# Attention to the context: a new order of scores, sums and fills on TensorE, with the sums of values kept in SBUF

## The chip, the cores and the metric

The kernel runs on one core of a Trainium2 chip. The metric is the device time of one execution in microseconds; lower is better. A time is the median of several runs; views of the profile come from one further execution.

## The reference

The model is a stack of four layers of attention to a context, self-attention and a feed-forward block on x, 2 x 256 tokens of 256 features in float32. The change touches the attention to the context of layers 0 and 1. The context has 2 x 4096 tokens. Layer 0, cut to what matters (layer 1 is the same with other weights, no biases, and a projection of the output):

```python
q = _split_heads(hidden_states @ q_w.T + q_b)      # 16 heads of 16 features
k = _split_heads(context @ k_w.T + k_b)
v = _split_heads(context @ v_w.T + v_b)
scores = jnp.einsum('bhqd,bhkd->bhqk', q, k) / jnp.sqrt(jnp.float32(HD))
mask = (attention_mask > 0)[:, None, None, :]
scores = jnp.where(mask, -jnp.inf, scores)
probs = jax.nn.softmax(scores, axis=-1)
ctx = jnp.einsum('bhqk,bhkd->bhqd', probs, v)
```

Layer 3 attends to the context in another way. It needs, for each context token, a projection of its features, a softmax of the powers of their logarithms and, for each head, the 11 largest of 16 features (`_topk_sparsify`). Then it sums features times context over all tokens:

```python
k = k @ Wk.T
k = _focus(k, focusing_factor)      # |.|, mean, softmax(log * factor)
kh = _topk_sparsify(_to_heads(k))   # 11 of 16
kv = jnp.einsum('bnc,bnd->bcd', kh / sqrt_l, vh / sqrt_l)
```

This does not depend on x, and the kernel does it in the loops of layers 0 and 1 (one batch each), beside their attention.

## The kernel before

A layer's loop has 8 units (2 batches, 4 chunks of 4 heads) of 16 steps each (`PER`). A unit goes twice over the keys of its 4 heads, which lie as 32 rows each in the 128 partitions. Its first pass, `first_scores` (L1145), multiplies queries by keys, 4 matmuls of 32 x 128 weights and 512 keys a step, and VectorE takes the maximum of each bank (L1163). When the unit is through, `shift_queries` puts the maximum of each query into a spare row of the queries. The second pass, `scores` (L1169), runs 18 steps behind (`PER + LAG`): scores by key, 8 matmuls of 32 x 128 weights and 256 queries, then on ScalarE three exponentials (L1188), two of 512 elements and one of 1024. `weigh` (L1190) runs another step behind: 8 matmuls with 128 x 32 weights (values) add into one PSUM bank over the whole unit, four heads in four column tiles; the sum is copied out after 16 steps (L1210). `inverses` and `normalize` (L1135) divide it. TensorE does each float32 matmul in two passes, so the profile counts two instructions for each.

Beside these, a step has at most one fill: `project_keys` (L1066, two key chunks in two column tiles of 64, 8 matmul instructions, copied by ScalarE and stored by DMA into the key tiles), `project_values` (L1108), `Focus.project` (L752, one or two tiles of 128 tokens, copied by ScalarE) or `Focus.add_up` (L782, the sum of features times context, added by VectorE at L793). The first and last of these use `Net.matmuls` (L184) with full 128 x 128 weights; so do the values.

What follows the features is done in small pieces. `magnitudes` (L632) makes four ScalarE instructions and one of GpSimd for each tile. `weigh` of `Focus` (L641) takes logarithms (two loads of ScalarE's tables around them), multiplies on GpSimd and takes exponentials. `sparsify` (L671) finds the rank of each feature by 45 VectorE instructions and a few around them.

PE, VectorE and ScalarE run in the order in which the program issues (`manual_schedule`, L468). In `attend` (L1013) a step issues: s1 with its maxima; the fill; pieces of the ranking; s2 with its exponentials; the magnitudes of the features taken; weigh of the step before; pieces of `Focus.weigh`. Where the fills and the pieces of ranking go is worked out by `plan` (L896) from deadlines (a key tile, a value tile is due before its step) and from a credit of VectorE time: a step has room for 2.0 us of ranking, or 2.75 with a long fill, less what else VectorE does in it.

PSUM has 8 banks: here 3 of `mm` (in turn for the two single banks of a pair of scores, and for fills), 2 pairs of `sc` (the other two banks of a set of scores), 1 of `acc` (the values' sum).

Of the kernel before, what the change touches and what calls it, by code (L numbers as in the profile page):

```python
# [9 lines left out]

# [9 lines left out]
F32 = mybir.dt.float32  # L20
# [50 lines left out]
class Net:  # L71
# [43 lines left out]
    def four(self, name):  # L115

        ones, pair = [self.mm(name) for _ in range(2)], self.sc(name)
        banks = [*ones, pair[:, 0], pair[:, 1]]
        return banks, [(0, ones[0].unsqueeze(1)), (1, ones[1].unsqueeze(1)), (2, pair)]
# [64 lines left out]
    def matmuls(self, out, pairs):  # L184

        for i, (lhsT, rhs) in enumerate(pairs):
            self.nc.tensor.matmul(out, lhsT=lhsT, rhs=rhs, start=i == 0, stop=i == len(pairs) - 1)  # L187

# [282 lines left out]
    def attend_to_context(self, a, x, q_bias, wq, wo, alive):  # L471
        tc = self.tc
        with self.stage():
            norm = self.center(self.halves(x))
            if not a.begun:
                a.beginning = a.begin(2)
                run(a.beginning, 1)
            a.take_queries(norm, wq, q_bias, alive)
        with (
            self.banks(mm=3, sc=2, acc=1),  # L480
            tc.tile_pool(name="xa_v", bufs=1, reuse_waits="tile") as vpool,
            tc.tile_pool(name="xa_p", bufs=1, reuse_waits="tile") as ppool,
            tc.tile_pool(name="focus", bufs=2, reuse_waits="tile") as fpool,
        ):
            a.attend(vpool, ppool, fpool)
        with self.stage():
            return a.give_back(x, wo)
# [124 lines left out]
class Focus:  # L612
# [139 lines left out]
    def project(self, kc, first, n=1):  # L752
# [12 lines left out]
        for i in range(n):  # L765
# [5 lines left out]
            net.matmuls(ps[:, i * D : (i + 1) * D], [(ctx[:, d, at], self.wk[:, d, :]) for d in range(ND)])  # L771
# [3 lines left out]
        yield  # L775
# [6 lines left out]
    def add_up(self, kc, m):  # L782
# [3 lines left out]
        ps = self.net.mm("kc_sum")[:, : D + 1]  # L786
        self.net.matmuls(ps, [(k[:, t, m * P : (m + 1) * P], self.tokens[:, t, :]) for t in range(NT)])
        yield
        kc_sum = self.kc[self.b][:, m, :]
# [4 lines left out]
        if m == ND - 1:  # L794
            self.load_tokens()


class ContextAttention:
# [36 lines left out]
    def begin(self, n):  # L835
# [5 lines left out]
        for j in range(n):  # L841
            run(self.project_keys(j))
            yield
# [52 lines left out]
    def plan(self):  # L896

        PER, LAG, n = self.PER, self.LAG, len(self.UNITS)  # L900
        STEPS = (n + 1) * PER + LAG + 2
        focus = self.net.focus
        fills, todo, kinds, last = {}, [], {}, n * PER
        self.done = {}

        short, full = 2.0, 2.75
        taken = [0.0] * (STEPS + 8)
        for u in range(n):
            at = PER * (u + 1)
            fills[at] = self.shift_queries(u)  # L910
            taken[at - 1] += 0.3
            taken[at] += 0.43
            at = PER * (u + 2) + LAG + 1
            self.done[at] = u
            taken[at - 1] += 0.43
            taken[at] += 0.25
            if u < n - 1:
                fills[at + 1] = self.normalize(u)
                taken[at + 1] += 0.43 if self.v_bias is None else 0.8

        for kc in range(NKC):
            first = 5 + 31 * kc // 2
            todo += [(first + 2 * t + 4, first + t, ("features", kc, t)) for t in range(NT)]
            todo += [(first + 29.5 + m, first + 14, ("sums", kc, m)) for m in range(ND)]
        for j in range(self.begun, n * NKC // 2):
# [3 lines left out]
            free = max(4 * j - 8, 2 * i + PER + LAG + 1 if i >= 0 else 0)  # L929
            todo.append((4 * j - (5 if j < NKC // 2 else 3), free + 1, ("keys", j)))  # L930
        for b in range(NB):
            for kc in range(NKC):
                for k2 in range(2):
                    i = b * NKC + kc - self.VALUE_TILES
                    free = (i // NKC + 1) * NC16 * PER + LAG + 2 * (i % NKC) + 2 if i >= 0 else -1
                    first = (b * NC16 + 1) * PER + LAG + 2 * kc + k2
                    todo.append((first, free + 1, ("values", b, kc, k2)))
        todo.sort()
        fixed = sorted(fills)
        make = dict(keys=self.project_keys, values=self.project_values, features=focus.project, sums=focus.add_up)  # L940
        self.weighings, self.rankings, costs = {}, {}, focus.costs()
        begin, over, logs, credit = {}, {}, set(), 0.0
        ranked, at, waiting = 0, 0, []
# [11 lines left out]
        def ready(g, deadline, earliest, which):  # L955
            kind, kc, *_ = which
            if earliest > g or (g in logs and kind != "sums" and deadline > g):
                return False
            if kind == "keys":

                return kinds.get(g - 1) != kind or deadline <= g
            if kind == "features":
                return kc < 3 or not any(w[:2] == ("sums", kc - 3) for _, _, w in todo)
            return kind != "sums" or over.get(kc, g) + 1 < g

        def pressed(g):

            for n, (deadline, _, _) in enumerate(todo):
                if n + 1 + sum(g < f <= deadline for f in fixed) > deadline - g:
                    return True  # L970
            return False

        for g in range(STEPS):
            room = short
            t = None if g in fills else next((t for t in todo if ready(g, *t)), None)
            if t is not None:
                todo.remove(t)
                kind, *which = t[2]
                kinds[g] = kind
                assert t[0] >= g or kind in ("features", "sums"), (g, t)  # L980
                fills[g] = make[kind](*which)
                if kind == "features":
                    kc, tile = which
                    if tile + 1 < NT and pressed(g):
                        todo.remove(next(t for t in todo if t[2] == ("features", kc, tile + 1)))
                        fills[g] = focus.project(kc, tile, 2)
                        room, tile = full, tile + 1
                    if tile == NT - 1:
                        waiting.append((kc, g))
                else:  # L990
                    room = full
                    taken[g] += 0.42 * (kind == "sums")

                    if kind == "sums" and waiting and waiting[0][1] < g - 1:
                        take_logs(g - 1)
            if g < PER:
                room = 0.5
            if g >= last + 1:
                room = 2.2
            if waiting and waiting[0][1] < g and (ranked == waiting[0][0] or ranked + 1 == waiting[0][0] and at >= 30):  # L1000
                take_logs(g)
            credit = min(credit, 0.5) + room - taken[g]
# [7 lines left out]
        assert not todo and ranked == NKC, (todo, ranked)  # L1010
        return fills

    def attend(self, vpool, ppool, fpool):  # L1013
# [12 lines left out]
        for g in range((n + 1) * PER + LAG + 2):  # L1026
            second = g - PER - LAG
            if g < n * PER:
                self.first_scores(g // PER, g % PER)
# [6 lines left out]
            run(fills.get(g, ()))  # L1036
# [5 lines left out]
            if 0 <= second < n * PER:  # L1042
                self.scores(second // PER, second % PER)
            focus.magnitudes_of_taken()
            if 0 <= second - 1 < n * PER:
                self.weigh((second - 1) // PER, (second - 1) % PER)
            if g in self.done:
                self.inverses = net.inverses(self.weighed)
                if self.done[g] == n - 1:
                    run(self.normalize(n - 1))  # L1050
# [15 lines left out]
    def project_keys(self, j):  # L1066
# [5 lines left out]
        dense = self.cpool.tile([P, KC], F32, name="k_dense", tag="k_dense")  # L1072
        ps = net.mm("k_ps")
        for d in range(ND):
            for i, ctx in enumerate(self.key_ctx[j]):
                nc.tensor.matmul(  # L1076
                    ps[i * HR : (i + 1) * HR, :],
                    lhsT=self.wk[:, d, c * HR : (c + 1) * HR],
                    rhs=ctx[:, d, :],
                    start=d == 0,  # L1080
                    stop=d == ND - 1,
                )
            if d < ND - 1:
                yield
        self.load_keys_ctx()
        if self.k_bias is None:
            nc.scalar.copy(dense, ps)
        else:
            nc.scalar.activation(dense, ps, AF.Identity, bias=self.k_bias[:, c : c + 1])
# [18 lines left out]
    def project_values(self, b, kc, k2):  # L1108

        net, nc = self.net, self.nc  # L1110
        if k2 == 0:
# [5 lines left out]
        for kk in range(2):  # L1117
            at = slice(kk * P, (kk + 1) * P)
            net.matmuls(ps[:, kk * D : (kk + 1) * D], [(ctx[:, d, at], self.wv[:, d, :]) for d in range(ND)])
            if kk == 0:  # L1120
                yield
        heads = v[:, 2 * k2 : 2 * k2 + 2, : H * VH].rearrange("p k (h e) -> p k h e", e=VH)
        nc.scalar.copy(heads[:, :, :, :DH], ps.rearrange("p (k h e) -> p k h e", k=2, e=DH))  # L1123
        self.load_values_ctx()

    def shift_queries(self, u):
# [5 lines left out]
        yield  # L1132
        nc.vector.tensor_tensor(self.q[u], self.q[u], ps[:, :S], ALU.add)

    def normalize(self, u):  # L1135
# [6 lines left out]
        yield  # L1142


    def first_scores(self, u, n):  # L1145
# [16 lines left out]
        for i, sc in parts:  # L1162
            nc.vector.tensor_reduce(mx[:, qt, i : i + sc.shape[1], kc], sc, AX.X, ALU.max)  # L1163
# [26 lines left out]
    def weigh(self, u, n):  # L1190
# [4 lines left out]
        if n == 0:  # L1195
            self.acc = self.net.acc("attn_acc")
        ps, v = self.weights.pop((u, n)), self.values[b, kc]
        for kk in range(2):
            for i in range(NG):
                at = (c * NG + i) * VH  # L1200
                nc.tensor.matmul(  # L1201
                    self.acc[i * HP : (i + 1) * HP, :S],
                    lhsT=v[:, 2 * k2 + kk, at : at + HP],
                    rhs=ps[:, i, kk * S : (kk + 1) * S],
                    start=n == kk == 0,
                    stop=n == self.PER - 1 and kk == 1,
                )
        if n == self.PER - 1:
            self.weighed = self.ppool.tile([P, S], F32, name="a", tag="a")
            nc.vector.tensor_copy(self.weighed, self.acc[:, :S])  # L1210
# [1160 lines left out]
```

## Time and profile before

| | before |
|---|---|
| median of 3 runs, us | 2444.99 (2443.58 to 2449.97) |
| profiled execution, us | 2444.92 |
| its span from first to last instruction, us | 2443.2 |
| PE busy, us (share) | 2288.8 (94%) |
| VectorE (DVE) busy | 1546.0 (63%) |
| ScalarE (ACT) busy | 1115.1 (46%) |
| GpSimd (POOL) busy | 347.3 (14%) |
| mean granted clock of TensorE | 0.966 |
| chain that ended last: PE, DVE, ACT | 56%, 5%, 3% |
| layer 0's loop: s1 alone, all three, without s1 | 65.1, 536.4, 49.4 us |
| layer 1's loop, the same | 55.7, 535.6, 48.9 us |

Busy time of PE counts pipelined matmuls, so a full PE is not one at its peak. A line of the groups has the source line, the engine, the operation, what it writes and reads, its shape and count, then busy time and mean ns of one, then the idle time of its engine ahead of it and what ended most of that. A line of the timeline has start, duration, engine, line, operation, shape and count. PEld is the load of weights, which runs beside PE.

### The profile page before, as it was taken

Reading aid. Unit: us, or ns where it says so; the run is one execution under the profiler, and the core shown is the slowest. Engines: PE = TensorE matmul, PEld = TensorE weight load, DVE = VectorE, ACT = ScalarE, POOL = GpSimd, SP = SyncE. Lnnn points to the kernel's source line nnn. Section 1 sums busy time; section 2 is a strip of 40 time slices with the busy share of each in tenths; the row PEclk is TensorE's granted clock in tenths of the full one; section 3 lists DMA queues with packets and bytes.
Section 4 is the critical chain, followed back from the end, with each engine's and each line's share of the span. In section 5 each row is a group of like instructions: output and inputs, shape, how many; then the busy total and the mean of one; then the engine's idle time right before and its main releaser. Section 6 shows DMA issues by size and latency. Waiting matters only on the chain.

```text
span 2443.2 us, 43313 instructions
## 1 busy us (share of the span) xinstructions
PE 2288.8 (94%) x17142; PEld 1228.1 (50%) x17142; DVE 1546.0 (63%) x2947; ACT 1115.1 (46%) x2185; POOL 347.3 (14%) x529
## 2 busy tenths in 40 slices
PE   7999999999999699999999999999999996899998
PEld 3454444544544365544454544564448453455453
DVE  4978988788746657978888778453331354444343
ACT  3466655655715334556566566641131252233232
POOL 4000001000024603000010010000011031003030
PEclk9999999999999799999999999999999997898989
DMA  6432232132011123332222221201323100000100
GB/s 200 147 98 86 93 97 93 54 114 67 10 39 36 50 95 120 102 97 92 93 92 93 76 89 41 79 23 52 100 94 95 43 19 14 35 21 12 59 12 22
DMA packets 97801, 174.45 MB, mean 71 GB/s; under 512 B 15120, under 2 KB 63888, under 8 KB 96704
## 3 DMA queue, kind: packets, MB, share of 16 engines
q1 hardware_dynamic: 97600, 171.68, 21.8%
q8 instruction: 137, 2.24, 0.4%
q14 instruction: 64, 0.52, 0.1%
HBM read 154.25 MB, written 0.59 MB: 63 GB/s over the span
## 4 chain that ended last, share of the span: by engine, by line
PE 56%; DVE 5%; ACT 3%; POOL 1%; issue 1%; DMA 0%; ACTq 0%; SPq 0%; DVEq 0%; POOLq 0%
PE s L1179 6%; PE s L1155 5%; PE proj L187 5%; PE attn_acc L1201 5%; PE v_ps L187 4%; PE expert L187 2%; PE k_ps L1076 2%; PE s L187 2%; PE c_acc L1799 2%; PE ffn_ps L187 2%; PE s L1476 1%; PE f_ps L187 1%; DVE mx L1163 1%; PE kc_sum L187 1%; PE kq_ps L187 1%; PE qk_ps L187 1%
## 5 line engine op out<-in xcount | busy, mean ns | idle before, releaser
L1163 DVE TENSOR_REDUCE mx<-s 128x1 f32<-128x512 f32 (+1 forms) x768 | 619.7, 863 | 189.6 <-PE s L1155 187.9
L1188 ACT ACTIVATE p<-s 128x512 f32<-128x512 f32 (+1 forms) x768 | 512.1, 740 | 233.6 <-PE s L1179 232.5
L1179 PE MATMUL s<-xa_q,xa_k 32*128 32x256 f32 x4096 | 338.4, 401 | 22.6 <-DVE mx L1163 22.6
L1155 PE MATMUL s<-xa_k,xa_q 32*128 32x512 f32 x2048 | 313.7, 640 | 5.7 <-ACT p L1188 3.6
L1179 PEld LDWEIGHTS s<-xa_q,xa_k 32*128 32x128 f32 x4096 | 212.9, 184 | 161.5 <-DVE mx L1163 104.1
L1201 PE MATMUL attn_acc<-p,xv 128*32 128x256 f32 x4096 | 277.7, 385 | 0.6 <-ACT p L1188 0.6
L1201 PEld LDWEIGHTS attn_acc<-p,xv 128*32 128x32 f32 x4096 | 111.9, 109 | 128.2 <-issue 83.2
L685 DVE TENSOR_TENSOR ge<-fy 128x960 bf16<-128x960 f32 (+14 forms) x240 | 169.6, 707 | 6.5
L639 POOL TENSOR_TENSOR fy<-fy,low 128x256 f32<-128x256 f32 x64 | 46.4, 725 | 844.5 <-ACT fy L638 844.5
L1155 PEld LDWEIGHTS s<-xa_k,xa_q 32*128 32x128 f32 x2048 | 88.7, 183 | 121.4 <-ACT p L1188 66.7
L687 DVE TENSOR_TENSOR rank<-rank,ge 128x960 bf16<-128x960 bf16 (+14 forms) x240 | 103.9, 433 | 6.0
L689 DVE TENSOR_TENSOR rank<-rank,ge 128x960 bf16<-128x960 bf16 (+14 forms) x240 | 100.9, 421 | 2.6
L395 POOL TENSOR_SCALAR p<-p,r 128x128 f32<-128x128 f32 (+1 forms) x192 | 82.5, 442 | 130.5 <-DVE r L391 70.6
L1123 ACT COPY xv<-v_ps 128x512 f32<-128x512 f32 x64 | 37.6, 587 | 115.7 <-PE v_ps L187 114.1
L376 ACT ACTIVATE p<-p,top 128x256 f32<-128x256 f32 (+1 forms) x128 | 57.1, 447 | 70.1 <-DVE top L364 68.9
L1076 PE MATMUL k_ps<-ctx_k,w_L0x_wk 128*64 128x512 f32 x256 | 66.7, 615 | 6.5 <-DMA ctx_k<-in_ctxT 6.1
L187 PE MATMUL f_ps<-f_wk,f_ctx 128*128 128x256 f32 x256 | 68.9, 400 | 0.6 <-DMA f_ctx<-in_ctxT 0.6
L187 PEld LDWEIGHTS f_ps<-f_wk,f_ctx 128*128 128x128 f32 x256 | 44.5, 189 | 43.2 <-ACT p L1188 19.0
L1799 PE MATMUL c_acc<-pT,ctx_n 128*128 128x256 f32 x256 | 62.0, 387 | 4.2 <-ACT pT L1772 3.0
L187 PE MATMUL v_ps<-w_L0x_wv,ctx_v 128*128 128x256 f32 x256 | 64.8, 397 | 0.0
L187 PE MATMUL kc_sum<-f_tok,fy 128*128 128x257 f32 x256 | 64.2, 393 | 0.0
L187 PE MATMUL v_ps<-w_L1x_wv,ctx_v 128*128 128x256 f32 x256 | 63.8, 392 | 0.0
(489 smaller groups left out, 3353.1 us busy)
## 6 DMA issues: line engine op xcount, KB each, us to landing
ctx_k<-in_ctxT SPq DMA_DIRECT2D x128, 512.0 KB
ctx_v<-in_ctxT SPq DMA_DIRECT2D x64, 256.0 KB
xa_k<-k_dense SPq DMA_DIRECT2D x512, 32.0 KB
f_ctx<-in_ctxT SPq DMA_DIRECT2D x32, 256.0 KB
f_tok<-in_ctx SPq DMA_DIRECT2D x16, 512.0 KB
ctxT<-in_ctxT SPq DMA_DIRECT2D x16, 512.0 KB
ctx_n<-in_ctx SPq DMA_DIRECT2D x16, 512.0 KB
xa_k<-key_masks SPq DMA_DIRECT2D x128, 8.0 KB
```

What stands on the lines that cost most here:

```text
L187: self.nc.tensor.matmul(out, lhsT=lhsT, rhs=rhs, start=i == 0, stop=i == len(pairs) - 1)
L395: nc.gpsimd.tensor_scalar(p[:, j, :nk], p[:, j, :nk], r[:, j : j + 1], 1.0, ALU.mult, ALU.mult)
L685: nc.vector.tensor_tensor(ge[:, :, :n], w[:, :, :n], w[:, :, P - n :], ALU.is_ge)
L687: nc.vector.tensor_tensor(rank[:, :, P - n :], rank[:, :, P - n :], ge[:, :, :n], ALU.add)
L689: nc.vector.tensor_tensor(rank[:, :, :n], rank[:, :, :n], ge[:, :, :n], ALU.subtract)
L1076: nc.tensor.matmul(ps[i * HR : (i + 1) * HR, :], lhsT=self.wk[:, d, c * HR : (c + 1) * HR], rhs=ctx[:, d, :], start=d == 0, stop=d == ND - 1,)
L1155: nc.tensor.matmul(banks[i], lhsT=self.q[u][rows, qt * P : (qt + 1) * P], rhs=k[rows, :], start=True, stop=True,)
L1163: nc.vector.tensor_reduce(mx[:, qt, i : i + sc.shape[1], kc], sc, AX.X, ALU.max)
L1179: nc.tensor.matmul(banks[i][:, kk * S : (kk + 1) * S], lhsT=k[rows, at], rhs=self.q[u][rows, :], start=True, stop=True,)
L1188: nc.scalar.activation(p[:, i : i + sc.shape[1], :], sc, AF.Exp, scale=DH**-0.5)
L1201: nc.tensor.matmul(self.acc[i * HP : (i + 1) * HP, :S], lhsT=v[:, 2 * k2 + kk, at : at + HP], rhs=ps[:, i, kk * S : (kk + 1) * S], start=n ...
L1799: nc.tensor.matmul(accs[m], lhsT=of[:, (k + i) % (KC // P), m * P : (m + 1) * P], rhs=pT[:, i, :], start=k + i == 0, stop=k + i == KT - 1,)
```

## The change

- The order of a step becomes: s2 with its exponentials; s1 with the maxima of its two single banks; weigh of the step before; the maximum of s1's pair of banks (a function of its own now); the fills; pieces of the ranking; magnitudes; pieces of `Focus.weigh`.
- The values, features and sums are multiplied by `by_columns`: each matmul with 128 columns of weights becomes four with 32, in four column tiles. The keys go in four tiles of 32 columns and not in two of 64.
- `weigh` takes an `mm` bank in each step, closes its sum there, and VectorE adds it to a tile in SBUF (a copy in a unit's first step). The bank of `acc` goes to `mm`, which has 4.
- A fill is cut into two parts (a half of the keys, one of two token tiles, a half of the columns of a sum); a step gets none, one or several of them, after the largest share of parts per step that any deadline asks for.
- The planner's VectorE room is 1.3 us in a step with s1 and 1.6 without, plus an `ease` that is raised by 0.02 until all pieces have a place. Features start at step 0 (before 5) and then every 16 steps (before 15.5).

The diff, cut (the planner to its rates, the fills to one of each sort):

```diff
+    def by_columns(self, out, pairs):
+
+        for i, (lhsT, rhs) in enumerate(pairs):
+            for g in range(NG):
+                cols = slice(g * HP, (g + 1) * HP)
+                self.nc.tensor.matmul(out[cols], lhsT=lhsT[:, cols], rhs=rhs, start=i == 0, stop=i == len(pairs) - 1)
...
-            self.banks(mm=3, sc=2, acc=1),
+            self.banks(mm=4, sc=2, acc=0),
...
-            net.matmuls(ps[:, i * D : (i + 1) * D], [(ctx[:, d, at], self.wk[:, d, :]) for d in range(ND)])
+            net.by_columns(ps[:, i * D : (i + 1) * D], [(ctx[:, d, at], self.wk[:, d, :]) for d in range(ND)])
...
-    def add_up(self, kc, m):
+    def add_up(self, kc, m, first, n=1):
...
+        cols = slice(first * P, (first + n) * P + first + n - 1)
+        ps = self.net.mm("kc_sum")[:, : cols.stop - cols.start]
+        self.net.by_columns(ps, [(k[:, t, m * P : (m + 1) * P], self.tokens[:, t, cols]) for t in range(NT)])
...
+        def rate(g):
+
+            most, parts = 0.0, 0
+            for deadline, _, _, _, part in todo:
+                parts += 2 - part
+                room = int(deadline) - g + 1 - sum(small[g : int(deadline) + 1])
+                most = max(most, parts / max(room, 0.5))
+            return most
...
+            due = min(due + rate(g), 3.0) if g >= PER else 2.0
+            k = int(due + 0.5 - small[g])
...
+                room = 1.3 if g < last else 1.6
...
+            credit = min(credit, 0.5) + room + ease - taken[g]
...
+            if 0 <= second < n * PER:
+                self.scores(second // PER, second % PER)
             if g < n * PER:
-                self.first_scores(g // PER, g % PER)
+                pair = self.first_scores(g // PER, g % PER)
...
-            run(fills.get(g, ()))
+            if 0 <= second - 1 < n * PER:
+                self.weigh((second - 1) // PER, (second - 1) % PER)
+            if g < n * PER:
+                self.finish_first_scores(g // PER, g % PER, pair)
+            for fill in fills.get(g, ()):
+                fill()
...
-            if 0 <= second < n * PER:
-                self.scores(second // PER, second % PER)
             focus.magnitudes_of_taken()
-            if 0 <= second - 1 < n * PER:
-                self.weigh((second - 1) // PER, (second - 1) % PER)
...
+                for row in (i * HR, i * HR + HP):
+                    col = c * HR + row % HR
+                    nc.tensor.matmul(
+                        ps[row : row + HP, :],
+                        lhsT=self.wk[:, d, col : col + HP],
+                        rhs=ctx[:, d, at],
+                        start=d == 0,
+                        stop=d == ND - 1,
+                    )
...
-        for i, sc in parts:
-            nc.vector.tensor_reduce(mx[:, qt, i : i + sc.shape[1], kc], sc, AX.X, ALU.max)
+        for i, sc in parts[:2]:
+            nc.vector.tensor_reduce(mx[:, qt, i : i + 1, kc], sc, AX.X, ALU.max)
+        return parts[2][1]
+
+    def finish_first_scores(self, u, n, pair):
+
+        nc, mx = self.nc, self.mx[u]
+        nc.vector.tensor_reduce(mx[:, n % 2, 2:, n // 2], pair, AX.X, ALU.max)
...
-        if n == 0:
-            self.acc = self.net.acc("attn_acc")
+        acc = self.net.mm("attn_acc")[:, :S]
...
+        if n == 0:
+            self.adding = self.ppool.tile([P, S], F32, name="a", tag="a", bufs=2)
+            nc.vector.tensor_copy(self.adding, acc)
+        else:
+            nc.vector.tensor_tensor(self.adding, self.adding, acc, ALU.add)
         if n == self.PER - 1:
-            self.weighed = self.ppool.tile([P, S], F32, name="a", tag="a")
-            nc.vector.tensor_copy(self.weighed, self.acc[:, :S])
+            self.weighed = self.adding
```

## Prediction

> **What bounds the kernel now.** I read the page's costliest groups first, then the timeline of PE inside the loop of the attention to the context, then the windows of its stretches, then the timeline of ACT and the waits. In the following I call one pass of the loop over `g` a step, its parts s1 (first scores, L1155), s2 (second scores, L1179), weigh (L1201) and fill (a projection or a sum of features, L187 or L1076).
>
> ```profile
> L1163 DVE TENSOR_REDUCE mx<-s 128x1 f32<-128x512 f32 (+1 forms) x768 | 619.7, 863 | 189.6 <-PE s L1155 187.9
> L1188 ACT ACTIVATE p<-s 128x512 f32<-128x512 f32 (+1 forms) x768 | 512.1, 740 | 233.6 <-PE s L1179 232.5
> L1179 PE MATMUL s<-xa_q,xa_k 32*128 32x256 f32 x4096 | 338.4, 401 | 22.6 <-DVE mx L1163 22.6
> L1155 PE MATMUL s<-xa_k,xa_q 32*128 32x512 f32 x2048 | 313.7, 640 | 5.7 <-ACT p L1188 3.6
> L1201 PE MATMUL attn_acc<-p,xv 128*32 128x256 f32 x4096 | 277.7, 385 | 0.6 <-ACT p L1188 0.6
> ```
>
> The idle times say who waits: DVE and ACT each wait about 190 and 234 us for PE, PE itself 29 us in all for them. PE sets the pace, DVE is the next.
>
> ```profile
> 28.10:93.20 65.10, 58.58 (x293) 27.54 (x290) 50.04 (x70) 21.23 (x48) 19.91 (x25) 1.00 0.60 187
> 93.20:629.60 536.40, 524.08 (x5069) 263.32 (x5070) 446.55 (x737) 321.43 (x586) 46.34 (x68) 1.00 0.27 85
> 629.60:679.00 49.40, 48.90 (x658) 29.62 (x658) 29.89 (x64) 39.55 (x65) 1.84 (x4) 1.00 0.04 12
> ```
>
> These are layer 0's three stretches (columns: length, then busy PE, PE weight loads, DVE, ACT, POOL, the clock, DMA): steps with s1 alone; the middle, about 109 steps of 4.92 us with s1, s2 and weigh; the end without s1. Layer 1 has 55.7, 535.6 and 48.9 us at the same clock, so I work with layer 0 and double. The middle is what the change can move: PE 524 of 536 us, DVE 447.
>
> ```profile
> 299.64 1.15 PE L1179 MATMUL s<-xa_q,xa_k 32*128 32x256 f32 x16
> 300.72 1.07 PE L1201 MATMUL attn_acc<-p,xv 128*32 128x256 f32 x16
> 301.72 1.14 PE L1155 MATMUL s<-xa_k,xa_q 32*128 32x512 f32 x8
> 302.79 1.99 PE L187 MATMUL v_ps<-w_L0x_wv,ctx_v 128*128 128x256 f32 x8
> 304.71 1.15 PE L1179 MATMUL s<-xa_q,xa_k 32*128 32x256 f32 x16
> ...
> 216.01 1.14 PE L1155 MATMUL s<-xa_k,xa_q 32*128 32x512 f32 x8
> 216.98 0.59 PE L1179 MATMUL s<-xa_q,xa_k 32*128 32x256 f32 x2
> ```
>
> One step takes 304.71 - 299.64 = 5.07 us: s2 1.08, weigh 1.00, s1 1.07, a fill of values 1.92, without a wait. The shape changes four times (32x128, 128x32, 32x128, 128x128). At 216 us s1 is followed by s2, the same shape: 0.97 us from start to start and not 1.07. That tenth is what the change is after.
>
> **The change, part by part.** *PE.* In the trace's single starts, s2's four groups of four stand at 304.714, 305.034, 305.250, 305.466, and weigh follows at 305.790. So a group takes 0.216, and a change of shape adds 0.104 behind the first group and 0.108 at the end. For weigh the same starts give 0.025 and 0.112, for s1 0.104 and 0.108 around two groups of 0.432. All three hold 0.864 us of matmuls. A fill of values holds 8 x 0.216 = 1.728 and pays 0.104 + 0.093.
>
> The new order is s2, s1 (one shape), weigh, fills in four column tiles (weigh's shape). With a whole fill a step is (0.104 + 0.864 + 0.864 + 0.108) + (0.025 + 0.864 + 1.728 + 0.112) = 4.67 us, 0.40 less. With half a fill it was 1.08 + 1.00 + 1.07 + 1.06 = 4.21 and becomes 3.80, also 0.40 less. A key fill was already column-tiled by 64 and took 1.87 on end: 0.35 less. Without a fill: 0.10 less. The middle stretch has 22 values, 14 sums and 23 features (59 in all), 25 keys, about 12 steps without: 59 x 0.40 + 25 x 0.35 + 12 x 0.10 = 33.5 us. PE would go from 536 to 503 us, and if the waits for the score banks that sit in it now (28 us, below) went too, to 475.
>
> Column tiles as fills: weigh is the very form that `by_columns` issues (128x32 weights, 256 moving columns), with other weights for each matmul, and its 16 weight loads fit into 1.00 us. So I add nothing for them. Bounds: halves of the sums move only 128 columns (nearest row: weigh's group, 0.216). If such a group could not go below 0.216, half a sum would cost 0.86 us more; with 16 sums, all halved, up to 32 x 0.86 = 28 us a layer. At the other end nothing, or a few us of gain. I take nothing, since those loads have the four column tiles of weigh too.
>
> [...] Weigh's row (4096 loads, 112 us busy in sum where 4096 x 0.109 would be 446) shows them overlapped; I go by the row.
>
> *Waits for banks.* s2 now waits up to 0.94 us in many steps whose fill is short, because it follows s1 closely and needs the banks that DVE still reduces: from the starts, some 24 us in the middle, plus 4 to 8 us behind the logarithms. After the change s2 leads s1, and its banks were reduced a step before. What is late next is DVE.
>
> *DVE.* The sum leaves PSUM each step: `tensor_tensor` 128x256 with one operand in PSUM, 0.41 us (L1138's form; L793, 128x257, 0.41), some 0.08 of it beside the next instruction (325.47 to 325.80 between starts). 108 weighs in the stretch, 7 of them copied already: 101 x 0.34 to 0.42 = 34 to 42; I take 38. DVE's need is 446.6 + 38 = 485 us. Its share was 0.98 in 986.5 to 1010 and 0.93 in 320 to 360, the fullest windows. At 0.97 it needs 500 us. So DVE takes PE's place as the bound: 503 or less against 500. The planner spreads the rankings by `ease` so that they last the whole loop; I count them unchanged (all 368 a layer must run).
>
> *ACT.* Its own work is the same, its place is not. Now the magnitudes and logarithms come behind the exponentials of the same step. After the change they stand behind the fill's copy at the end of a step, and ahead of the next exponentials. s2 and s1 together take the four `mm` banks once round, so weigh always gets the bank of s2's first part and waits for the first exponential of its own step. Nominal slack: exponentials start 1.16 after s2 (136.10 against 134.94), 0.60 long, so 1.82 with the signal; weigh is due at 1.94.
>
> ```profile
> 135.08 0.69 ACT L1089 ACTIVATE k_dense<-k_ps,vectors 128x512 f32<-128x512 f32 x1 [1.43 <-PE k_ps L1076]
> 136.10 2.00 ACT L1188 ACTIVATE p<-s 128x512 f32<-128x512 f32 x3 [0.33 <-PE s L1179]
> 138.12 1.28 ACT L646 ACT_TABLE_LOAD   x1
> 139.41 1.15 ACT L646 ACTIVATE fy<-fy,eps 128x1024 f32<-128x1024 f32 x1
> 140.58 1.28 ACT L649 ACT_TABLE_LOAD   x1
> 141.87 0.20 ACT L649 ACTIVATE ready<-eps 128x1 f32<-128x1 f32 x1
> 141.98 1.98 ACT L1188 ACTIVATE p<-s 128x512 f32<-128x512 f32 x3
> ```
>
> Here a key copy starts 0.14 behind its fill, and a block of logarithms takes 3.95 us. Behind a fill's copy (0.14 + 0.6) it would end 4.7 us after the step and the exponential at 5.3, weigh being due at 1.94: 3.3 us late, 7 times a middle. Magnitudes of one tile (1.0 us, 123.01 to 124.07) make weigh 0.2 late, of two (2.0, 108.72 to 110.72) 1.4, each of the two pairs of exponentials of a chunk (1.1 us behind a copy) 0.45. With 14 single and 7 double features in a middle: 7 x 3.3 + 14 x 0.2 + 7 x 1.4 + 14 x 0.45 = 42 us on PE. DVE has up to 1.9 us of rankings per step to work off meanwhile; beyond that only the logarithms reach: 7 x (3.3 - 1.9) = 10 us. So the middle is 500 + 10 = 510.
>
> *The rest.* First stretch: s1 and fill 2.94 for 2.995, 16 times: 0.9 us. The end stretch, DMA volume, POOL and SP keep their work; key stores are due some four steps ahead as now. I count nothing there (bounds: 5 us either way in layer 0's first stretch, where 8 us of DMA waits lie).
>
> **Sum.** Per layer 536.4 - 510 + 0.9 = 27.3; two layers 55. The profiled execution took 2444.92 us (span 2443.2 and 1.7 around it), the median of the runs is 2444.99. 2444.9 - 55 = 2390.
>
> **Rivals.** *DVE and PE fit together better* (0.22): the blocks on ACT are absorbed and DVE runs at 0.98: 495 us, which is over PE's 475. Gain 2 x (41.4 + 0.9) = 85: 2360. For it: 24 us of bank waits are structural and go. Against: no window over 24 us shows such a share.
>
> *The gain is half eaten* (0.13): half of the 42 us reaches the loop: 500 + 21 + 10 of present waits = 531, gain 2 x 6 = 12: 2433.
>
> *ACT between fill and weigh* (0.13), on the slower side: the sum waits for weigh, the second maximum stands behind the sum on DVE, and the next s1 waits for that bank. A late exponential then stops PE and DVE together. With DVE at 0.95 (510) and all 42 us on top: 552, or 2 x 15 more: 2475. It decides once waits exceed 36 us a layer over 500.
>
> *It doesn't do what it says* (0.02): column fills pay a change each (84 x 0.25 = 21 us on PE): 503 + 21 = 524, 2420.
>
> **Numbers.** Forecast 2390 with 0.50 (2370 to 2415). No change is within 0.3% (2437.7 to 2452.3), about what a measurement of this kernel can tell. Faster: 0.50 + 0.22 + 0.05 + 0.02 = 0.79; within: 0.08 of the half-eaten case, 0.01 of the slower; slower 0.12. The range 2345 to 2440 leaves out the slower rival and the edges.
>
> **What would show it.** A whole step at 4.67 where nothing waits, s2 to s1 at 0.97; by DVE's share near 0.95 and PE's idle growing "<-DVE"; weigh with waits for `p` behind the logarithms. The prediction is wrong if the middle stays at 530 us or more (ACT), if column groups exceed 0.216 us, or if DVE's additions cost over 0.42.

## The result and the profile after

| | before | after |
|---|---|---|
| median, us (4 runs each) | 2444.28 (2441.45 to 2449.97) | 2476.49 (2471.34 to 2481.89) |
| ratio, 95% interval | | 1.0129 (1.0098 to 1.016): slower |
| profiled execution, its span, us | 2444.92, 2443.2 | 2481.89, 2480.2 |
| PE, DVE, ACT busy, us | 2288.8, 1546.0, 1115.1 | 2281.2, 1619.6, 1120.7 |
| mean granted clock of TensorE | 0.966 | 0.951 |
| layer 0's loop, layer 1's loop, us | 655.9, 644.6 | 667.1, 658.5 |
| the rest of the program, us | 1142.7 | 1154.7 |

A loop is counted here from its first s1 to the projection behind it. The kernel became slower by 1.3%, and 25.1 of the 37 us between the two profiled executions lie in the two loops. The rest runs the same code but for four key fills. In the kernels of this study it takes 1135 to 1157 us, with no order that follows an edit. It follows the clock: the rest holds between 142 us at half clock (in the two kernels of 1135 us) and 190 us (in the one of 1157), before 162 and after 179. At 0.50 weigh's groups of four matmuls start 0.427 us apart (from 219.00 in the changed kernel), at 1.00 0.216 (from 207.32). With half of the time at half clock taken off, the rest of all eleven kernels lies between 1061.5 and 1064.9 us. So, by that measure, some 8.5 of the 12 us by which it grew here are half clock. Executions of one kernel differ the same way: the changed one took 2471.34 us at a mean clock of 0.955 and 2481.89 at 0.951. Below I therefore compare loops, and medians for the whole.

The page's costliest groups of the changed kernel (columns: busy us, mean ns of one, then idle time of the engine just before the group and what ended it):

```profile
L1192 DVE TENSOR_REDUCE mx<-s 128x1 f32<-128x512 f32 x512 | 329.4, 683 | 93.6 <-PE s L1184 92.5
L1184 PE MATMUL s<-xa_k,xa_q 32*128 32x512 f32 x2048 | 365.9, 619 | 6.0 <-ACT xv L1153 4.2
L1235 PE MATMUL attn_acc<-p,xv 128*32 128x256 f32 x4096 | 283.3, 392 | 59.9 <-ACT p L1223 59.1
...
L1246 DVE TENSOR_TENSOR a<-a,attn_acc 128x256 f32<-128x256 f32 x240 | 99.1, 413 | 62.9 <-PE attn_acc L1235 62.5
```

Three things are to be seen. Weigh's idle time was 0.6 us before; now it is 59.9 us, ended by ScalarE's exponentials. First scores keep PE busy for 365.9 us where it was 313.7, with as many matmuls and fewer ns for one: where they start one by one, as their banks come free, the profile counts PE as busy in between (below, the 7 that begin at 610.49 are spread over 2.22 us; the 8 at 214.73, with no wait, take 1.04). So waits within s1 hide in PE's busy time. And VectorE, which was to be the bound, waits 62.9 us for weigh ahead of its additions.

The middle stretches (all three parts in a step) of layers 0 and 1 in the windows of the changed kernel (length; busy PE, PEld, DVE, ACT, POOL; clock, DMA share, GB/s):

```profile
97.37:643.25 545.88, 515.85 (x6744) 272.94 (x6748) 468.10 (x818) 320.23 (x592) 43.41 (x60) 0.97 0.28 86
1011.30:1550.35 539.05, 508.92 (x6648) 267.09 (x6652) 465.74 (x811) 315.18 (x583) 43.56 (x60) 0.98 0.28 85
```

They were 536.4 and 535.6, were forecast at 510, and are 545.9 and 539.1. VectorE is busy for 0.86 of them, not 0.97. PE's 0.94 holds the waits within s1. So no engine is full: the time went into waits of one engine for another.

**Where it waits for ScalarE.** PE's timeline around one block of logarithms:

```profile
211.92 1.91 PE L194 MATMUL v_ps<-w_L0x_wv,ctx_v 128*32 128x256 f32 x32
213.76 1.15 PE L1214 MATMUL s<-xa_q,xa_k 32*128 32x256 f32 x16
214.73 1.04 PE L1184 MATMUL s<-xa_k,xa_q 32*128 32x512 f32 x8
219.00 1.94 PE L1235 MATMUL attn_acc<-p,xv 128*32 128x256 f32 x16 [3.23 <-ACT p L1223]
220.86 1.69 PE L1214 MATMUL s<-xa_q,xa_k 32*128 32x256 f32 x16
```

And ScalarE's in the same place:

```profile
213.90 0.59 ACT L1153 COPY xv<-v_ps 128x512 f32<-128x512 f32 x1 [1.73 <-PE v_ps L194]
214.50 1.28 ACT L653 ACT_TABLE_LOAD   x1
215.80 1.15 ACT L653 ACTIVATE fy<-fy,eps 128x1024 f32<-128x1024 f32 x1
216.96 1.28 ACT L656 ACT_TABLE_LOAD   x1
...
218.37 1.98 ACT L1223 ACTIVATE p<-s 128x512 f32<-128x512 f32 x3
```

The scores of s2 are in PSUM at about 215, but ScalarE takes the fill's copy and then the block that was issued behind it, and begins the exponentials at 218.37. Weigh, due at 215.7, starts at 219.00: 3.3 us late. It does not wait for what it multiplies: the exponentials of the step before were through at 212.17. It waits for its bank, which held the first part of s2 and is free when the first exponential ends (at 218.94). Behind it PE is slow: weigh to s2 takes 1.86 us instead of 1.00, s2 to s1 1.53 instead of 0.97. The windows of three stretches show why (the last three columns are the clock, the DMA share and GB/s):

```profile
215.00:218.50 3.50, 0.77 (x8) 0.00 (x0) 2.11 (x5) 3.46 (x5) 1.12 (x1) 1.00 0.27 80
218.60:222.00 3.40, 3.00 (x28) 1.58 (x32) 1.00 (x2) 1.74 (x3) 0.00 (x0) 0.50 0.00 0
222.00:225.40 3.40, 3.40 (x44) 1.64 (x40) 3.33 (x9) 2.00 (x3) 0.00 (x0) 1.00 0.02 2
```

The stretch in which PE waits has the clock at 1.00, the next 3.4 us have 0.50, then it is 1.00 again. So such a wait can be paid a second time, behind it. Within the loops PE had 3.4 us at half clock before and has 61.4 now.

**Where it waits for VectorE.** VectorE's timeline in a step without a fill, late in layer 0's loop:

```profile
608.79 1.28 DVE L1192 TENSOR_REDUCE mx<-s 128x1 f32<-128x512 f32 x2
609.99 0.41 DVE L1246 TENSOR_TENSOR a<-a,attn_acc 128x256 f32<-128x256 f32 x1
610.32 1.22 DVE L1198 TENSOR_REDUCE mx<-s 128x2 f32<-128x1024 f32 x1
611.45 0.61 DVE L694 TENSOR_TENSOR rank<-rank,ge 128x896 bf16<-128x896 bf16 x1
612.10 0.62 DVE L696 TENSOR_TENSOR rank<-rank,ge 128x896 bf16<-128x896 bf16 x1
```

And PE's in the same step:

```profile
608.30 1.07 PE L1235 MATMUL attn_acc<-p,xv 128*32 128x256 f32 x16
609.30 1.15 PE L1214 MATMUL s<-xa_q,xa_k 32*128 32x256 f32 x13
...
610.49 2.22 PE L1184 MATMUL s<-xa_k,xa_q 32*128 32x512 f32 x7
612.64 1.07 PE L1235 MATMUL attn_acc<-p,xv 128*32 128x256 f32 x16
```

VectorE has no gap: maxima, sum and two pieces of ranking fill 608.79 to 612.64. PE would need 2.94 us for this step (weigh 1.00, s2 0.97, s1 0.97) and takes 4.34 (weigh starts at 608.30 and again at 612.64), as s1's last matmuls wait for the pair of banks that L1198 frees (it ends at 611.54; the next of them starts at 611.59). In such steps VectorE is the bound: over the two middles it stands idle for 9% of the time in steps without a fill, and for 18 to 26% in steps with a whole fill or more. Of the middle's 109 steps, 36 and 37 have no fill in the changed kernel (counted from PE's matmuls, layers 0 and 1); the kernel before had 25. The 12 of the prediction and the 29 that is written ahead of an experiment below are smaller.

To size these waits I took every step of the middle from the single starts of matmuls (110 steps a layer, mean of both). From s2's first pass to s1's last it takes 1.42 us where nothing waits, from there to weigh 0.52: together 213 us for 110 steps. What is longer I count as a wait, for VectorE's banks in the first part and for ScalarE in the second:

| us per layer | waits in s1 | waits of weigh | weigh, fills and the rest | at half clock (lies in all three) |
|---|---|---|---|---|
| after | 49.8 | 32.1 | 246.1 | 23.9 |
| `e1_act_behind` | 51.2 | 11.4 | 247.8 | 10.2 |
| `e2_no_sum` | 34.3 | 33.5 | 246.6 | 25.6 |
| `e4_no_logs` | 49.7 | 16.4 | 245.1 | 10.2 |
| `e6_room_by_fill` | 41.1 | 31.2 | 247.2 | 20.5 |
| `e7_max_before_sum` | 50.4 | 31.5 | 246.2 | 23.9 |
| `e8_all_three` | 43.6 | 8.9 | 250.0 | 15.4 |
| `e10_three_no_sum` | 25.2 | 12.3 | 246.4 | 8.5 |

So the changed kernel's middle is 213 + 246 + 50 + 32 = 541 us. Without waits it would be 459.

### The profile page after: what moved, and what is told of

It reads as the page before. It is cut to its first block, busy times and chain, and to the rows that moved or that the text cites. A ratio compares the mean times of both kernels' runs of the same rounds, so it can differ in the third digit from the quotient of the medians.

```text
span 2480.2 us, 51919 instructions
## 1 busy us (share of the span) xinstructions
PE 2281.2 (92%) x21270; PEld 1233.5 (50%) x21270; DVE 1619.6 (65%) x3198; ACT 1120.7 (45%) x2222; POOL 352.6 (14%) x529
## 4 chain that ended last, share of the span: by engine, by line
PE 52%; DVE 6%; ACT 5%; POOL 2%; issue 1%; DMA 0%; SPq 0%; ACTq 0%; DVEq 0%; POOLq 0%
PE proj L187 5%; PE attn_acc L1235 5%; PE s L1184 4%; PE s L1214 4%; PE expert L187 2%; PE s L187 2%; PE c_acc L1837 2%; PE k_ps L1107 2%; PE v_ps L194 2%; PE ffn_ps L187 2%; PE s L1514 1%; PE v_ps L187 1%; PE kq_ps L187 1%; PE qk_ps L187 1%; PE moe_acc L1726 1%; PE kc_sum L194 1%
## 5 line engine op out<-in xcount | busy, mean ns | idle before, releaser
L1192 DVE TENSOR_REDUCE mx<-s 128x1 f32<-128x512 f32 x512 | 329.4, 683 | 93.6 <-PE s L1184 92.5
L1184 PE MATMUL s<-xa_k,xa_q 32*128 32x512 f32 x2048 | 365.9, 619 | 6.0 <-ACT xv L1153 4.2
L1235 PE MATMUL attn_acc<-p,xv 128*32 128x256 f32 x4096 | 283.3, 392 | 59.9 <-ACT p L1223 59.1
L1214 PE MATMUL s<-xa_q,xa_k 32*128 32x256 f32 x4096 | 319.6, 410 | 4.6 <-DVE mx L1192 2.5
L1198 DVE TENSOR_REDUCE mx<-s 128x2 f32<-128x1024 f32 x256 | 311.5, 1217 | 0.0
L1184 PEld LDWEIGHTS s<-xa_k,xa_q 32*128 32x128 f32 x2048 | 140.9, 188 | 83.7 <-DVE mx L1198 43.7
L1246 DVE TENSOR_TENSOR a<-a,attn_acc 128x256 f32<-128x256 f32 x240 | 99.1, 413 | 62.9 <-PE attn_acc L1235 62.5
L1153 ACT COPY xv<-v_ps 128x256 f32<-128x256 f32 (+1 forms) x93 | 42.2, 453 | 100.7 <-PE v_ps L194 100.6
L1107 PE MATMUL k_ps<-ctx_k,w_L0x_wk 128*32 128x512 f32 (+1 forms) x624 | 69.6, 536 | 6.5 <-DMA ctx_k<-in_ctxT 5.2
L194 PE MATMUL kc_sum<-f_tok,fy 128*32 128x257 f32 (+2 forms) x1376 | 63.8, 331 | 3.1 <-POOL fy L703 3.1
L1107 PE MATMUL k_ps<-ctx_k,w_L1x_wq 128*32 128x512 f32 (+1 forms) x592 | 63.6, 548 | 1.0 <-ACT conv L1349 1.0
```

The costliest lines, as they stand in the source:

```text
L194: self.nc.tensor.matmul(out[cols], lhsT=lhsT[:, cols], rhs=rhs, start=i == 0, stop=i == len(pairs) - 1)
L1107: nc.tensor.matmul(ps[row : row + HP, :], lhsT=self.wk[:, d, col : col + HP], rhs=ctx[:, d, at], start=d == 0, stop=d == ND - 1,)
L1184: nc.tensor.matmul(banks[i], lhsT=self.q[u][rows, qt * P : (qt + 1) * P], rhs=k[rows, :], start=True, stop=True,)
L1192: nc.vector.tensor_reduce(mx[:, qt, i : i + 1, kc], sc, AX.X, ALU.max)
L1198: nc.vector.tensor_reduce(mx[:, n % 2, 2:, n // 2], pair, AX.X, ALU.max)
L1214: nc.tensor.matmul(banks[i][:, kk * S : (kk + 1) * S], lhsT=k[rows, at], rhs=self.q[u][rows, :], start=True, stop=True,)
```

## The experiments

Theory A: ScalarE's logarithms, magnitudes and exponentials of features now stand between a fill's copy and the next step's exponentials, so weigh waits, and half clock follows. Theory B: VectorE, with the additions and the rankings in every step, holds s1. All kernels start from the changed one. The loops of each (one profiled execution), in us:

| | both loops | against after | ratio to before, 95% interval |
|---|---|---|---|
| before | 1300.5 | | 1 |
| after | 1325.6 | | 1.0129 (1.0098 to 1.016) |
| `e1_act_behind` | 1291.0 | -34.6 | 0.9982 (0.9967 to 0.9996) |
| `e2_no_sum` | 1294.9 | -30.7 | 0.9977 (0.9961 to 0.9994) |
| `e4_no_logs` | 1288.8 | -36.8 | 0.9966 (0.9943 to 0.999) |
| `e5_warm` | 1321.2 | -4.4 | 1.0104 (1.0077 to 1.013) |
| `e6_room_by_fill` | 1304.2 | -21.4 | 0.9987 (0.9973 to 1.0) |
| `e7_max_before_sum` | 1325.0 | -0.6 | 1.0081 (1.0057 to 1.0105) |
| `e8_all_three` | 1276.6 | -49.0 | 0.9873 (0.9846 to 0.99) |
| `e9_three_full_fills` | 1271.0 | -54.6 | 0.9874 (0.982 to 0.9928) |
| `e10_three_no_sum` | 1230.9 | -94.7 | 0.9719 (0.969 to 0.9748) |

### ScalarE's blocks behind the exponentials: `e1_act_behind`

```diff
                 self.scores(second // PER, second % PER)
+            focus.magnitudes_of_taken()
+            for kc in self.weighings.get(g - 1, ()):
+                run(focus.weighing[kc], 1)
             if g < n * PER:
...
-            focus.magnitudes_of_taken()
...
-            for kc in self.weighings.get(g, ()):
-                run(focus.weighing[kc], 1)
```

> The changed kernel with one move: the magnitudes and the pieces of Focus.weigh of a step are issued behind the exponentials of the next step, not ahead of them. Theory A (ScalarE's work between the fill and the next weigh stops TensorE, and waits over some 3 us halve its clock for a while): the waits behind magnitudes go (some 16 us a layer), those behind logarithms shrink and with them most of the 15 us at half clock: about 2400 (2385 to 2435), weigh's idle time '<-ACT p' at most half. Theory B (VectorE, which now adds the sums, is the bound): 2465 to 2480.

Measured: 2444.05 us, ratio 0.9982; both loops 34.6 us shorter. As many instructions run on every engine; only the place of these pieces in the order differs, on ScalarE above all. Weigh's row of the groups in this kernel:

```profile
L1235 PE MATMUL attn_acc<-p,xv 128*32 128x256 f32 x4096 | 282.6, 391 | 22.2 <-ACT p L1223 22.0
```

The idle time falls from 59.9 to 22.2 us, and the waits in s1 stay (49.8 and 51.2 a layer). So A is a cause, worth some 36 us by the two ratios to the kernel before, and not the only one: the time lies outside the ranges of both theories, and the middles are 525.5 and 524.1 us, not 510.

### No additions: `e2_no_sum`

```diff
-        if n == 0:
+        if n == (0 if self.layer == 0 else self.PER - 1):
             self.adding = self.ppool.tile([P, S], F32, name="a", tag="a", bufs=2)
             nc.vector.tensor_copy(self.adding, acc)
-        else:
-            nc.vector.tensor_tensor(self.adding, self.adding, acc, ALU.add)
```

> The changed kernel without the additions of the sums on VectorE: one step of each unit is copied, the others are left out, so the result of the attention is not the reference's. Theory B: VectorE's need falls by some 40 us a layer, and the time to about 2396. Theory A: TensorE still waits for ScalarE in the same places, 2455 to 2475.

Measured: 2443.51 us, ratio 0.9977. It lies between the two theories' numbers. Taking 99 us of additions off VectorE shortens the loops by 30.7 us; the waits in s1 fall by 15.5 us a layer, those of weigh stay at 33.5. Each theory holds part of the loss.

### No logarithms: `e4_no_logs`

```diff
-        nc.scalar.activation(y, y, AF.Ln, bias=self.eps)
-
-        ready = self.net.sm(1, name="ready", tag="ready")
-        nc.scalar.activation(ready, self.eps, AF.Exp)
```

> The changed kernel without the logarithm of the features and the two loads of ScalarE's tables around it (the powers are taken of the plain magnitudes, so the ranking and the sums of features are not the reference's). Theory A: eight blocks of 3.95 us a layer go, with their waits (some 20 us a layer) and nearly all the half clock (13 us a layer): about 2410 (2395 to 2425). Theory B: 2465 to 2480.

Measured: 2439.91 us, ratio 0.9966. The logarithms and their table loads are half of weigh's waits (32.1 to 16.4 us a layer); what is left is not theirs (magnitudes and exponentials of features stand in the same place; no run takes them alone). That is less than A alone would give, and again the waits in s1 do not move (49.7).

### Matmuls in place of the wait: `e5_warm`

```diff
-                self.scores(second // PER, second % PER)
+                self.scores(second // PER, second % PER, 4 if g in self.logs else 1)
...
-        for kk in range(2):
+        for kk in [0, 1] * times:
```

The second scores of the steps behind a block of logarithms are multiplied four times over, so that PE works while it would wait.

> The changed kernel with the second scores' matmuls issued four times over in the one step behind each block of logarithms: 2.6 us of repeated work, the same result, done while TensorE would wait for ScalarE. If the halved clock is a cost of its own, the idle stretches get too short to set it off and the loops have next to none of the 30 us each: 2450 to 2465 in spite of 40 us more of matmuls. If it is not, the time is the same or up to 20 us longer: 2476 to 2496.

Measured: 2473.79 us, ratio 1.0104 (1.0077 to 1.013) beside the changed kernel's 1.0129 (1.0098 to 1.016): the intervals overlap. Time at half clock in the loops falls from 61.4 to 23.9 us, and the loops are 4.4 us shorter although 14 x 2.6 = 36 us of matmuls were added (4768 second scores instead of 4096, so 14 steps with 48 more). The time lies between the two ranges. So half clock follows the waits and most of it can be avoided, but this kernel only bounds its price from below, by some 4 us: the added matmuls reach beyond the waits they fill. From the other side an estimate: where weigh's groups take 0.427 us for 0.216, at most half of the time at half clock is lost, 31 of the 61.4 us in the two loops.

### Rankings where there are fills: `e6_room_by_fill`

```diff
-                room = 1.3 if g < last else 1.6
+                room = 0.4 + 0.8 * done if g < last else 1.6
```

`done` counts the halves of fills in the step; the `ease` that the planner then needs is 0.44 where it was 0.50.

> The changed kernel with one line of the planner: the room for rankings on VectorE is 0.4 us plus 0.8 for each half of a fill in the step, and not 1.3 in every step (ease then comes out at 0.44, before 0.50). Theory C (the loop has 29 steps a layer without a fill in its middle, which are short on TensorE and as full as the others on VectorE, so that the next first scores wait there for the second maximum, 36 us a layer): over half of that goes, 2420 to 2450. Theory A (ScalarE alone is to blame): 2465 to 2480.

Measured: 2444.87 us, ratio 0.9987. The loops are 21.4 us shorter, the waits in s1 41.1 us a layer instead of 49.8, with weigh's as before (31.2). The time is in theory C's range, but only 8.7 us a layer of the waits went, where over half of 36 was expected. VectorE's busy time in the middle is much the same (471 us against 467), and in the steps without a fill it now idles for 19%, in those with a whole one or more for 8 to 10%. So it matters where the rankings stand, and not only that they run. The new plan moves fills too, though: the middle has 28 and 27 steps without one instead of 36 and 37, so the 21 us are the price of both.

### The pair's maximum ahead of the sum: `e7_max_before_sum`

```diff
-            if 0 <= second - 1 < n * PER:
-                self.weigh((second - 1) // PER, (second - 1) % PER)
             if g < n * PER:
                 self.finish_first_scores(g // PER, g % PER, pair)
+            if 0 <= second - 1 < n * PER:
+                self.weigh((second - 1) // PER, (second - 1) % PER)
```

> The changed kernel with the second maximum issued ahead of weigh and its sum on VectorE. If the sum's place ahead of it holds back the next first scores (0.41 us, and more where weigh is late), the waits of s1 fall by some 10 us a layer: 2450 to 2462. If VectorE is merely late as a whole, the sum takes the same time behind the maximum and nothing is won: 2468 to 2480.

Measured: 2464.44 us, ratio 1.0081, but the loops are unchanged (1325.0 against 1325.6 us): in the profiled executions the difference lies wholly in the rest of the program, where this edit changes nothing and 142 us instead of 179 are at half clock. The median lies between the two ranges; the waits of s1 do not fall (50.4 against 49.8 us a layer). The sum that waits for weigh, with the pair's maximum queued behind it, is therefore no cause of its own: VectorE has the same work in either order.

### All three, and what still holds it: `e8_all_three`, `e9_three_full_fills`, `e10_three_no_sum`

The first holds the edits of `e1_act_behind`, `e6_room_by_fill` and `e7_max_before_sum`. The second is the first with values, features and sums by full 128 x 128 weights again (`matmuls` for `by_columns`, three lines). The third is the first without the additions, by the diff of `e2_no_sum`.

> The three moves together: ScalarE's magnitudes and logarithms behind the next exponentials, rankings by the fill, the second maximum ahead of the sum. Theories A and C together (two separate causes whose prices add): 2390 to 2425, faster than the kernel before. If they hide one another (what ScalarE no longer holds back VectorE does): 2430 to 2445.

> The kernel with the three moves, its values, features and sums multiplied with full 128x128 weights again (the keys stay in four column tiles). If column tiles are worth the changes of shape that they spare, each step with such a fill pays 0.2 us more (0.108 and 0.104 between weigh and fill), some 55 steps a layer: 22 us more, 2438 (2430 to 2446). If TensorE only waits less for VectorE instead, 2412 to 2425. If column tiles cost more than full weights (loads that don't overlap), it is faster: under 2410.

> The kernel with the three moves without VectorE's additions of the sums (one step of each unit is copied, the others are left out, so the attention's result is not the reference's). If VectorE still holds back the first scores (some 43 us of waits a layer in the loops' middle), a good part of its 38 us goes: 2375 to 2395. If TensorE's own work and ScalarE are what is left: 2405 to 2418.

Measured: `e8_all_three` takes 2415.96 us, ratio 0.9873 (0.9846 to 0.99); it beats both kernels. The loops are 49.0 us shorter than the changed kernel's, where the edits alone gave 34.6 + 21.4 = 56.0: nearly additive, as was expected of two separate causes. Its middles, in the windows:

```profile
98.15:615.79 517.64, 503.63 (x6824) 266.58 (x6828) 468.83 (x823) 319.46 (x592) 41.24 (x60) 0.99 0.29 90
983.88:1500.19 516.31, 503.87 (x6856) 267.95 (x6860) 467.26 (x818) 315.02 (x591) 41.70 (x60) 0.98 0.29 90
```

VectorE's share is 468 / 517 = 0.91. Without the additions (`e10_three_no_sum`, 2380.85 us, ratio 0.9719) they are:

```profile
92.74:595.72 502.98, 488.86 (x6824) 263.72 (x6828) 438.65 (x722) 319.41 (x592) 41.58 (x60) 0.99 0.30 93
959.16:1452.79 493.63, 481.19 (x6856) 263.45 (x6860) 434.85 (x716) 314.93 (x591) 42.04 (x60) 1.00 0.31 94
```

Of VectorE's work 31 us a layer are gone, and the stretch is 15 and 23 us shorter; the waits in s1 fall from 43.6 to 25.2. Time at half clock in the two loops falls too, from 51.2 to 23.9 us, which by the same estimate can be at most 14 of the 46 us. So VectorE still holds `e8_all_three`, and its additions of the sum to SBUF are a price that the change pays there.

`e9_three_full_fills` takes 2418.22 us, ratio 0.9874 (0.982 to 0.9928), the same as with column tiles. The intervals leave room for some 15 us between the two, but hardly for the 22 us expected. A step of its PE timeline:

```profile
205.94 1.07 PE L1235 MATMUL attn_acc<-p,xv 128*32 128x256 f32 x16
206.94 1.99 PE L187 MATMUL v_ps<-w_L0x_wv,ctx_v 128*128 128x256 f32 x8
208.87 1.15 PE L1214 MATMUL s<-xa_q,xa_k 32*128 32x256 f32 x16
```

Weigh to fill to s2 is 1.00 + 1.93 us here, 0.89 + 1.84 with column tiles: the 0.20 us are real, but they do not show in the time. The profiled executions can't narrow it: the loops of `e9_three_full_fills` are 5.6 us shorter, with 20.5 us at half clock in them where `e8_all_three` had 51.2.

## Why the prediction was wrong, point by point

**PE's shapes: right.** s2 to s1 is 0.97 us (213.76 to 214.73), a whole column-tiled fill 1.84 and weigh ahead of it 0.89; with s1 to weigh at 0.97 that is the 4.67 us of the working. The halved sums did no harm: 8 groups of 128 columns start within 0.79 us (from 246.00), 0.11 us for a group, below the bound of 0.216. The loop without waits, forecast at 475 us, is 459, half clock included; I did not trace these 16 us further, but fills that share a step pay no change between them: a whole one with another behind it takes 1.72 us (244.28 to 246.00), one ahead of s2 the 1.84. That the weight loads of these column tiles add nothing is right too: the fill at 211.92 holds 32 matmul instructions with a load of 0.11 us each, 3.5 us end to end, and takes 1.84 us in all. The loads run beside one another (1.04 us of busy PEld) and beside the matmuls: the first four start at 211.71, with weigh's last four matmuls and ahead of the fill's first at 211.92. In the kernel before, weigh's 4096 loads of 109 ns kept PEld busy for 111.9 us.

**DVE's additions: right in size.** 413 ns each against the 0.41 us used, 120 a layer.

**ScalarE's blocks: right in size, wrong in what reaches the loop.** Here is the main failed step: "beyond that only the logarithms reach: 7 x (3.3 - 1.9) = 10 us", of 42. The block shown makes weigh 3.3 us late, the very number of the working, and 32 us a layer reach the loop where 10 were let through; `e1_act_behind` takes 21 of them away by moving ScalarE's blocks alone. The working let VectorE catch up on rankings while PE stands. But a step has only its own pieces of ranking to catch up on, and when these are through VectorE stands too (it waits 62.9 us for weigh ahead of its additions, in both loops). In steps where PE is the bound, being ahead with VectorE's work should win nothing either; that is argued, not measured.

**VectorE's bound: wrong by an average.** "At 0.97 it needs 500 us" took a window of the fullest work for the whole loop. The s1 waits put this term at 459 + 50 = 509. The rankings did not stay where they were either ("I count them unchanged"): of the middle's 322 pieces 25 a layer moved out of it, most of them behind it, so VectorE is busy there for 468 and 466 us where 485 was worked out, and yet the loop waits for it for 50 us a layer. The planner gives each step with s1 the same room for ranking, while the length of steps became uneven: in steps without a fill VectorE is the bound, in those with a whole one or more it has gaps. The sum over steps of the slower engine is more than the slower of the two sums. The plan of `e6_room_by_fill`, with rankings where the fills are, won 21 us without less work; even `e8_all_three` reaches a share of 0.91 only.

**Half clock: not in the working at all.** It lies in the numbers above: 23.9 us a layer in the middle, by the estimate above at most 12 us of loss. In the rows at 215.00 and 218.60 PE starts nothing for 3.82 us (215.18 to 219.00), and 3.40 us at 0.50 follow. Shorter waits were followed by half clock too: four of 2.37 to 2.90 us were, and one of 3.65 us was not. It should have been priced for each late weigh of 3.3 us, though not every one of them pays (last section).

**Beside the middle.** I counted the other stretches as little changed. The rankings of the last chunk now end late, at 692.5 us, behind the last weigh (before at 664.0, 16 us ahead of its end), so the last sums and the projection come 4.5 and 6.5 us later, and layer 1's first stretch is 4.8 us longer, with a wait of 4.16 us for a copy of values and half clock behind it.

**The rivals.** "ACT between fill and weigh" at 2475 us names the mechanism that `e1_act_behind` takes away, and its number is near the 2476.5 measured, in part by luck. Its middle of 552 us is above the 545.9 and 539.1 measured, while the tails, the first stretch of layer 1 and the rest of the program add what the middle lacks. Its order of events on VectorE, the sum holding the pair's maximum, has no effect of its own (`e7_max_before_sum`). By its own point of decision, 36 us of waits over 500, the 32 us of ScalarE alone would not have done; with the 9 us of VectorE over 500 they do.

What stays open: the price of half clock by itself, between 4 and 31 us in the two loops, and why the rest of the program has more of it in one execution than in another. No run gives weigh a bank that ScalarE does not have to free, so how much of its wait comes from the shared banks and how much from ScalarE's order is not told apart.

## What to carry over

When work is put in another order, ask for each long block on each engine what is now queued behind it and when that was due; a block that was free behind the exponentials cost 3.3 us ahead of them. Compare engines step by step and not by sums over a loop: where steps are uneven, movable work belongs into the long ones, and the planner that spreads it has to know which they are. A shape change saved on TensorE need not show while another engine holds the loop: column-tiled fills saved 0.20 us each, and the time without them was the same, as far as some 15 us can be told.

## What the runs showed of the hardware beside

In the two middles of the changed kernel half clock comes in pieces of 3.41 us, twice two of them on end (6.83 us). 16 times PE starts nothing there for 2.37 to 4.73 us; 12 of these are followed by one or two pieces at 0.50, which begin between 2.0 us ahead of the end of the wait and 1.6 us behind it. The other four, one of 3.65 us among them (to 496.45), are not, while another of 3.65 us (to 1405.52) is: in these runs length alone does not decide, and the "over some 3 us" written ahead of `e1_act_behind` is not shown as a bound. Column tiles of 32 columns with new weights for each matmul run four in 0.216 us in the changed kernel (the fill of values from 211.92), like one full matmul of 256 columns in the kernel before (the fill of values from 302.79).
